# Moving one constant and padding it, so that every tile read by TensorE starts at a multiple of 1024 (or 512) bytes

## The chip, the cores and the metric

The kernel runs on one core of a Trainium2 chip. The metric is the device time of one launch in microseconds (us); lower is better. The engines are named as in the profile: PE is TensorE (its weight loads are shown apart as PEld), DVE is VectorE, ACT is ScalarE, POOL is GpSimd, SP is SyncE, which here only issues DMAs. SBUF is the on-chip memory; an address in it is counted in bytes within a partition.

## The reference

There are 128 samples `x[b]` of 128 tokens by 512 features in float32, and one adjacency matrix `adj` of 128 by 128.

```
# layer 0
A = adj @ x ;  C = A + b ;  out = max over n of relu(A + (C - A))      # b per token
x = layernorm(x + out)
# layer 1: attention with 8 heads of 64, masked where adj == 0
q, k, v = x @ w_qkv
p = softmax(mask(q k^T / 8)) ;  o = (p v) @ w_proj + b_proj
x = layernorm(x + o + layernorm(o) * gamma + beta)
```

## The kernel before

The samples go in 32 groups of four. Products in which precision matters (the `dense` products of q, k and v, and the projection `po`) are done with fp32r operands: each operand is split into a high part, a low part and a difference (`x_h`, `x_l`, `x_d` for the activations, `w_h`, `w_l`, `w_d` for the qkv weights, `p_h`, `p_l`, `p_d` for the projection, `oh`, `ol`, `od` for the attention output). One product is 12 matmuls of 128 x 512: eight by `product` (L342, L343) and four by `product_d` (L350). A group has 12 `dense` products, called (g, j): j = 0 to 3 are v of the four samples, with the activations stationary and the weights moving; j = 4 to 11 are q and k, with the weights stationary and the activations moving. It also has four projections ('o', b), with `oh`, `ol`, `od` stationary and `p_h`, `p_l`, `p_d` moving. So there are 16 x 12 = 192 fp32r matmuls for a group. In the last eight projections the attention output is written into the then unused storage of `w_h`, `w_l`, `w_d`, so there the stationary operand lies in the weight tiles.

The other products are plain float32: `conv` (L186, `adjT` stationary, the sample `xt` moving), `scores` (L397), `attend` (L477, which reads the transposed weights `eT` and `v`).

Around the products DVE splits (L294, L296), adds the `product_d` parts (L381, L523), masks scores (L413) and normalizes softmax (L440); ACT does the exponentials (L431), copies two 16-bit planes of the softmax (L446) and of the normalized sample (L277), squares (L529); POOL makes differences (L308), the residual (L500, L501, L518) and the small arithmetic of the norms (L535, L536, L541, L544, L250). A transposition goes through DRAM: the planes are written (L450, L279) and read back by a transposing DMA into `eT` (L455) or `xT` (L283). SP issues nearly all DMAs from one queue, in order.

The order on every engine is fixed beforehand: each step gets a place by hand-set offsets (the table `O`), the steps are sorted by place, and each engine runs its own in that order and waits on semaphores. The order in a steady group on PE is: dense 4 and 5, two convs, dense 6, 8, 7, 11, 10, 9, then attend and scores, dense 0, po 0, dense 1, po 1, scores and attend, dense 2, dense 3, po 2, two convs, po 3.

Where a tile lies follows from the order in which the pools ask for it. The constant pool comes first: four small constants of the framework end at byte 16,512, then `b0_sb`, `ident`, `adjT`, `mask`, the nine weight tiles, `gamma_sb`, `bias_sb`, `beta_sb`, `mhalf` and `square`, each rounded up to 32 bytes. The pools for samples, groups and work follow without gaps. All tiles in them are multiples of 1024 bytes, down to the small statistics at the end.

Of the kernel before, what the change touches and what calls it, by code (L numbers as in the profile page):

```python
# [8 lines left out]
FP = mybir.dt.float32  # L9
# [17 lines left out]
def tile_adj_resnorm_d2(  # L27
# [39 lines left out]
    P = 128  # L67
    assert T == P and D == 512 and B % 4 == 0
    G = 4
# [6 lines left out]
    const = ctx.enter_context(tc.tile_pool(name="const", bufs=1))  # L76
# [15 lines left out]
        xs[b] = xt  # L92


    adj_sb = work.tile([P, D], FP, tag="xh", name="adj_sb")[:, :P]
    nc.scalar.dma_start(adj_sb, adj)
    b0_sb = const.tile([P, 1], FP, name="b0_sb")
# [67 lines left out]
    gamma_sb = const.tile([P, D], FP, name="gamma_sb")  # L165
    bias_sb = const.tile([P, D], FP, name="bias_sb")
    beta_sb = const.tile([P, D], FP, name="beta_sb")
    mhalf = const.tile([P, G], FP, name="mhalf")
    nc.vector.memset(mhalf, -0.5)
    square = const.tile([P, D], mybir.dt.bfloat16, name="square")  # L170

# [727 lines left out]
```

## Time and profile before

| what | value |
|---|---|
| median of 3 runs | 1971.6 us (1968.35 to 1975.02) |
| span of the profiled execution | 1967.2 us |
| PE busy, matmuls | 1872.0 us, 95% |
| DVE, ACT, POOL busy | 84%, 79%, 63% |
| TensorE clock granted, mean | 0.989 |
| from one steady group to the next (start of dense 4 of group 16 to that of group 17) | 974.67 to 1033.57, 58.90 us |

The profile gives the profiled execution by its span, from the first instruction to the last; its own time around the span is not given, and the median of the runs is 4.4 us above the span. In timelines a row has the start, the duration, engine, source line, operation, output and inputs, and the count if several are merged; a bracket gives idle time before it and what ended it. Ends of matmuls are modelled, so a row's duration is longer than its share of the stream; the distance from one start to the next is what a matmul costs there. Queue rows of SP (SPq) tell when a DMA was issued, not how long it ran.

### The profile page before, as it was taken

What the parts mean: (1) busy time and instruction counts of PE and PEld (TensorE: products, weight loads), DVE (VectorE), ACT (ScalarE), POOL (GpSimd) and SP (SyncE); (2) the same over time, 40 slices, a digit from 0 to 9 for tenths busy, and PEclk for the clock granted to TensorE, in tenths of its full rate; (3) what the DMA queues carried; (4) which work ended last, traced back from release to release, by engine and by line L of the source; (5) the groups of instructions that cost most, each with busy time, mean ns of one, the idle gap of its engine ahead of it and who ended that gap; (6) DMA issues with size and microseconds to landing.
All of it is one profiled execution on the core that took longest, in us unless ns stands there. A gap on an engine that the chain in (4) does not pass through costs nothing.

```text
span 1967.2 us, 33044 instructions
## 1 busy us (share of the span) xinstructions
PE 1872.0 (95%) x10569; PEld 1438.1 (73%) x10569; DVE 1648.1 (84%) x2585; ACT 1547.6 (79%) x3926; POOL 1246.0 (63%) x1935
## 2 busy tenths in 40 slices
PE   7799999999999999999999999999999999999995
PEld 4677777777777777777777777777777777777774
DVE  7778888888888888888888888888888888888875
ACT  4688878788878788878788878788878788878764
POOL 3256666666666666666666666666667666667667
PEclk9899999999999999999999999999999999999997
DMA  4366565666565666555666555766555666555641
GB/s 130 102 156 163 152 157 147 175 172 164 152 159 147 172 172 162 153 158 149 173 172 166 151 156 147 175 171 166 151 160 145 173 172 164 153 156 146 154 114 52
DMA packets 486141, 302.92 MB, mean 154 GB/s; under 512 B 399440, under 2 KB 403664, under 8 KB 485968
## 3 DMA queue, kind: packets, MB, share of 16 engines
q1 hardware_dynamic: 485104, 299.70, 57.2%
q8 instruction: 84, 1.38, 0.3%
q10 hardware_dynamic: 864, 1.12, 0.2%
q14 instruction: 89, 0.73, 0.1%
HBM read 72.16 MB, written 131.07 MB: 103 GB/s over the span
## 4 chain that ended last, share of the span: by engine, by line
PE 70%; POOL 11%; DVE 9%; issue 5%; ACT 3%; DMA 3%; SPq 0%; POOLq 0%; ACTq 0%; DVEq 0%
POOL x_d L308 5%; PE psc L397 5%; PE pav L477 5%; PE pa L186 3%; POOL od L308 2%; DMA eT<-rows 2%; DVE x_l L296 1%; DVE v L381 1%; POOL sum L536 1%; DVE xh L294 1%; ACT oh L303 1%; DVE o L523 1%; DVE o L548 1%; DVE o L509 1%; ACT x_h L303 1%
## 5 line engine op out<-in xcount | busy, mean ns | idle before, releaser
L431 ACT ACTIVATE e<-e,nmax 128x128 f32<-128x128 f32 x1016 | 393.1, 389 | 62.5 <-DVE nmax L422 62.5
L446 ACT COPY planes<-e 128x2048 uint16<-128x2048 uint16 x124 | 234.7, 1893 | 21.6 <-DVE e L440 21.5
L529 ACT ACTIVATE square<-o,sum 128x512 bf16<-128x512 f32 x256 | 183.1, 715 | 63.8 <-DVE o L523 62.8
L535 POOL TENSOR_SCALAR sum<-sum 128x1 f32<-128x1 f32 (+1 forms) x287 | 58.3, 203 | 269.8 <-ACT square L529 256.6
L501 POOL TENSOR_TENSOR xb<-xb,beta_sb 128x512 f32<-128x512 f32 x128 | 210.6, 1646 | 10.7
L308 POOL TENSOR_TENSOR x_d<-x_h,x_l 128x512 fp32r<-128x512 f32 x97 | 125.7, 1310 | 134.6 <-DVE x_l L296 74.9
L536 POOL TENSOR_TENSOR sum<-sum,mhalf 128x1 f32<-128x1 f32 (+1 forms) x287 | 181.1, 631 | 23.9
L431 ACT ACTIVATION_READ_ACCUMULATOR e<-e,nmax 128x1 f32 x1016 | 190.9, 188 | 0.0
L518 POOL TENSOR_TENSOR xb<-xb,o 128x512 f32<-128x512 f32 x125 | 164.6, 1317 | 4.9
L440 DVE TENSOR_TENSOR e<-e,sums 128x1024 f32<-128x1024 f32 x128 | 162.3, 1268 | 4.4
L548 DVE SCALAR_TENSOR_TENSOR o<-o,sum,gamma_sb 128x512 f32<-128x512 f32 x128 | 99.3, 776 | 76.5 <-POOL xb L518 72.9
L413 DVE SCALAR_TENSOR_TENSOR e<-psc,mask 128x1024 f32<-128x1024 f32 x127 | 151.8, 1216 | 3.3 <-ACT planes L446 2.7
L422 DVE TENSOR_REDUCE nmax<-e 128x8 f32<-128x1024 f32 x127 | 153.5, 1209 | 0.1
L477 PE MATMUL pav<-eT,v 128*64 128x128 f32 x2048 | 140.1, 280 | 11.4 <-DMA eT<-rows 5.4
L556 ACT ACTIVATE o<-o,sum 128x512 f32<-128x512 f32 x128 | 103.1, 807 | 54.6 <-POOL sum L544 54.6
L397 PE MATMUL psc<-qkT 64*128 64x128 f32 x2048 | 141.8, 284 | 2.5 <-DVE qkT L381 2.5
L500 POOL TENSOR_SCALAR xb<-xb,sum 128x512 f32<-128x512 f32 x128 | 120.8, 944 | 35.3 <-DMA xb<-in_x_dram 33.9
L397 PEld LDWEIGHTS psc<-qkT 64*128 64x128 f32 x2048 | 123.4, 189 | 25.9 <-issue 21.4
L259 ACT ACTIVATE xt<-xt,sum 128x512 f32<-128x512 f32 x127 | 102.4, 806 | 46.3 <-POOL sum L250 45.2
L477 PEld LDWEIGHTS pav<-eT,v 128*64 128x64 f32 x2048 | 110.8, 137 | 37.3 <-issue 15.4
L277 ACT COPY xplanes<-xt 128x1024 uint16<-128x1024 uint16 x124 | 129.7, 1046 | 5.1 <-DMA rowsx<-xplanes 1.2
L186 PE MATMUL pa<-xt,adjT 128*128 128x512 f32 x256 | 123.6, 607 | 6.9 <-ACT v L325 3.5
(4668 smaller groups left out, 5606.3 us busy)
## 6 DMA issues: line engine op xcount, KB each, us to landing
rows<-planes SPq DMA_DIRECT2D x124, 512.0 KB, 3.3
xt<-in_x_dram SPq DMA_DIRECT2D x128, 256.0 KB, 3.0
xb<-in_x_dram SPq DMA_DIRECT2D x128, 256.0 KB, 3.0
out_dram<-o SPq DMA_DIRECT2D x128, 256.0 KB, 2.8
rowsx<-xplanes SPq DMA_DIRECT2D x124, 256.0 KB, 2.4
wraw<-in_L_gnn_w_qkv_dram SPq DMA_DIRECT2D x8, 256.0 KB, 2.9
xT<-rowsx SPq DMA_TRANSPOSE x124, 3.6
eT<-rows SPq DMA_TRANSPOSE x124, 4.7
```

Source lines behind the costliest of these rows:

```text
L186: nc.tensor.matmul(pa[b], adjT, xs[b], start=True, stop=True)
L308: engine.tensor_tensor(fd, fh.bitcast(FP), fl.bitcast(FP), op=ALU.subtract)
L397: nc.tensor.matmul(psc[:, s, hp, :], qkT[hs, hp, i, :], qkT[hs, KC + hp, i, :], start=not with_mask, stop=not with_mask or hp == HP - 1,)
L422: nc.vector.tensor_reduce(nmax, src, AX.X, ALU.max, negate=True)
L431: nc.scalar.activation(e[:, j, :], src[:, j, :], AF.Exp, bias=nmax[:, j : j + 1], scale=1.0 if src is e else scale, accum_out=sums[:, j : ...
L440: nc.vector.tensor_tensor(e, e, sums[:, :, None].to_broadcast([P, H, P]), op=ALU.mult)
L446: nc.scalar.copy(planes, e.rearrange("p h m -> p (h m)").bitcast(U16).rearrange("p (m s) -> p s m", s=2),)
L477: nc.tensor.matmul(pavs[b][s * HD : (s + 1) * HD, hp, :], v[:, h * HD : (h + 1) * HD], eT[:, s * HP + hp, :], start=True, stop=True,)
L501: nc.gpsimd.tensor_tensor(xbs[b], xbs[b], beta_sb, op=ALU.add)
L518: engine.tensor_tensor(xbs[b], xbs[b], os[b], op=ALU.add)
L529: nc.scalar.activation(square, x, AF.Square, bias=s[:, 0:1], scale=-float(D), accum_out=s[:, 1:2],)
L536: nc.gpsimd.tensor_tensor(s, s, mhalf[:, :n], op=ALU.pow)
```

## The change

`mhalf`, a constant of four floats a partition that POOL uses as an exponent, is taken from the constant pool first and with 88 floats (352 bytes) instead of four (which took 32 with rounding); the code uses the first four as before. Nothing else is changed: the same instructions stand in the same order on every engine, with the same waits.

```
+    mhalf = const.tile([P, 88], FP, name="mhalf")[:, :G]
     adj_sb = work.tile([P, D], FP, tag="xh", name="adj_sb")[:, :P]
     ...
     beta_sb = const.tile([P, D], FP, name="beta_sb")
-    mhalf = const.tile([P, G], FP, name="mhalf")
     nc.vector.memset(mhalf, -0.5)
```

The addresses that follow from it:

| tile | start before | its remainder by 1024 and by 64 | start after | remainder by 1024 |
|---|---|---|---|---|
| `ident` | 16,544 | 160, 32 | 16,896 | 512 |
| `adjT` | 17,056 | 672, 32 | 17,408 | 0 |
| `w_h` | 18,080 | 672, 32 | 18,432 | 0 |
| `w_l`, `w_d`, `p_h`, `p_l`, `p_d` | 42,656 and on | 672, 32 | 43,008 and on | 0 |
| `gamma_sb`, `bias_sb`, `beta_sb` | 116,384 and on | 672, 32 | 116,736 and on | 0 |
| the sample tiles `xt` | 123,584 and on | 704, 0 | 123,904 and on | 0 |
| `x_h`, `x_l`, `x_d` | 131,776 and on | 704, 0 | 132,096 and on | 0 |
| `v`, `qkT`, `eT`, `oh`, `ol`, `od`, and the other work tiles | 156,352 and on | 704, 0 | 156,672 and on | 0 |

The weights and other constants move up by 352 bytes and everything behind them by 320. Slices of a tile that TensorE takes start at multiples of 512 bytes within it. So before, an operand in the weight tiles starts 32 bytes past a multiple of 64, and one in the group and work tiles at a multiple of 64; after, both start at multiples of 512. Among the group and work tiles the distances stay as they are.

## The prediction

> **What bounds the kernel now.** I read the page's first part and its chain first, then PE's timeline near the end and in a steady group, then the waits, and last the timelines of ACT, SP and DVE around the place where PE waits.
>
> ```profile
> span 1967.2 us, 33044 instructions
> ...
> PE 1872.0 (95%) x10569; PEld 1438.1 (73%) x10569; DVE 1648.1 (84%) x2585; ACT 1547.6 (79%) x3926; POOL 1246.0 (63%) x1935
> ...
> PE 70%; POOL 11%; DVE 9%; issue 5%; ACT 3%; DMA 3%; SPq 0%; POOLq 0%; ACTq 0%; DVEq 0%
> ```
>
> PE is busy 95% and holds 70% of the chain. The change touches no instruction, so it can only act on how long one takes, and the first question is whether any row depends on addresses. PE's timeline near the end has one that does. There the projection of sample 120 follows a dense product without a stop, and its stationary operand lies in the weight tiles:
>
> ```profile
> 1892.13 0.40 PE L342 MATMUL pm_(31, 1)_19611<-w_h,x_h 128*128 128x512 f32 x1
> ...
> 1893.99 1.10 PE L350 MATMUL pd_(31, 1)_19612<-w_d,x_d 128*128 128x512 f32 x4
> 1894.93 0.39 PE L342 MATMUL pm_('o', 120)_19626<-p_h,w_h 128*128 128x512 f32 x1
> ...
> 1896.74 1.07 PE L350 MATMUL pd_('o', 120)_19627<-p_d,w_d 128*128 128x512 f32 x4
> ```
>
> From 1892.13 to 1894.93 twelve matmuls start: 233 ns each. Their operands are 32 bytes apart modulo 64 (weights at 672 modulo 1024, activations at 704 or 192). From 1894.93 to 1896.74 eight start: 226 ns each. Their operands are both 672 or 160 modulo 1024, so equal modulo 64. Shape, type and count are the same, and the step changes with the first matmul of the new kind. Taking all of the trace's steps under 245 ns by this distance, at least 8 matmuls after the last stop, those 32 apart stand at 231 to 235, mean 233.3, in over 4,000 cases; those 0 apart at 226 and 227 as a rule, in some 25. All of the latter are near the end. It is not the idleness there: dense products at 1907, with no DMA in flight, still step by 231 and 235. Just after a stop the 0-apart ones lose the advantage for a while: the first four average 231.5, the next four 229.
>
> **The change, part by part.** The memory set and the pow that use `mhalf` keep size and order: nothing. The plain float32 products have no such excess to lose:
>
> ```profile
> 1027.56 1.88 PE L186 MATMUL pa<-xt,adjT 128*128 128x512 f32 x4
> ```
>
> Four of them in 1.88 us, of which one takes 0.59: (1.88 - 0.59) / 3 = 430 ns from start to start, for two passes each. One pass at full clock is 213 (rows at half clock, around 1913 us, step by 427 for a single one). Its operands are 32 apart today, and it pays only some 3 ns for two passes. Scores and attend read tiles whose distance stays. So does everything that DVE, ACT and POOL read, but for mask, gamma, bias and beta; there the add of beta (L501, 32 apart) comes down to 1.28 us in the steady group, as the add of `o` (L518, 0 apart) with 1.29, so I take 0 for these.
>
> That leaves the 6,120 fp32r matmuls. The last eight projections, 96, are 0 apart already; 6,024 change. After it all distances are 0 or 512 modulo 1024, as in the rows of sample 120, so each should go from 233.3 to 226.7: 6.6 ns. If all of it reached the end it would be 6,024 x 6.6 = 40 us. It cannot: before 114 us and after 1888 us other engines hold the chain, and a steady group has a stretch from the last matmul of dense 3 to po 3 in which POOL holds it, with 24 fp32r matmuls inside (PE idles 1.02 us there, below). For 30 groups 30 x 168 x 6.6 = 33 us is the most.
>
> Here a rule weighs against the change. The Trainium skill, "SBUF — State Buffer", section "Who interferes with whom", gives PE two independent read ports, one for the moving operand and one for the weight load, and says that PE never waits on anyone; by that the distance of the two starts could not matter and the sum would be 0. The rows above differ by 7 ns, and the rows decide.
>
> **Where the gain stops.** The steady group's turning points:
>
> ```profile
> 1015.46 2.20 PE L477 MATMUL pav<-eT,v 128*64 128x128 f32 x32
> ...
> 1023.45 1.10 PE L350 MATMUL pd_(16, 3)_10518<-w_d,x_d 128*128 128x512 f32 x4
> 1024.66 0.50 PE L342 MATMUL pp_('o', 62)_10543<-p_h,oh 128*128 128x512 f32 x1
> ...
> 1032.32 1.20 PE L350 MATMUL pd_('o', 63)_10606<-p_d,od 128*128 128x512 f32 x4 [1.02 <-POOL od L308]
> 1033.57 0.47 PE L342 MATMUL pp_(17, 4)_10644<-x_h,w_h 128*128 128x512 f32 x1
> ```
>
> ```profile
> PE pav L477 <- DMA eT<-rows: 5.2, 10, 0.9
> ```
>
> The second line is from PE's waits between 300 and 1800 us. In 10 of some 26 groups PE already arrives too early at the fourth attend and waits for the transposed `eT`; in the group shown it arrives about when `eT` lands. So PE may be faster in the 42 us from dense 4 to that attend (about 160 of the 192 matmuls) and only wait longer for `eT`, unless `eT` comes earlier too. ACT and SP tell when it comes:
>
> ```profile
> 1000.14 0.81 ACT L259 ACTIVATE xt<-xt,sum 128x512 f32<-128x512 f32 x1 [1.44 <-POOL sum L250]
> ...
> 1010.35 1.05 ACT L277 COPY xplanes<-xt 128x1024 uint16<-128x1024 uint16 x1
> ```
>
> ```profile
> 1011.42 0.34 SPq L279 DMA_DIRECT2D rowsx<-xplanes  x1
> 1011.86 2.13 SPq L455 DMA_TRANSPOSE eT<-rows  x1
> ```
>
> ```profile
> 1023.39 1.22 DVE L413 SCALAR_TENSOR_TENSOR e<-psc,mask 128x1024 f32<-128x1024 f32 x1
> ...
> 1026.83 0.69 DVE L296 TENSOR_TENSOR ol<-pav,xh_('o', 63)_10562 128x512 fp32r<-128x512 f32 x1 [1.03 <-PE pp_('o', 62)_10543 L343]
> ```
>
> `eT` of the fourth attend is issued at 1011.86, because SP is in order and its queue stood behind the write of the sample planes at 1011.42, which waits for ACT's copy of 1010.35; with the median 4.7 us from issue to landing (the page's DMA issues) it lands at 1016.56, just when that attend starts. ACT works without a break from 1000.14 to there, and started on POOL's norm. Followed further back in the same timelines: POOL from 983.2, on the residual's sample loaded (3.0 us) from 980.25; DVE from 967.9 to 980.2; and DVE's split at 967.9, like the one at 1026.83, waits for the last main matmul of po 2, which reads the single buffer `ol`. So there is a second circle of one group's length, through DVE, SP, POOL, DVE, ACT, POOL, ACT, SP and PE, and of PE's fp32r matmuls it holds only dense 2, dense 3 and eight of po 2: 24 + 8 = 32. They give 32 x 6.6 = 0.21 us a group. Besides, po 2 starts at 1024.66, while dense 3 ends at 1023.45 + 4 x 0.233 = 1024.38: 0.28 us, spent on DVE's masking (1023.39 + 1.22 = 1024.61), which frees the PSUM buffer. That row stands behind DVE work that PE feeds, so up to 0.28 can go too. Between 0.21 and 0.49 us a group I take the middle, 0.35: 30 x 0.35 = 10.5 us. The rest of PE's 1.27 us turns into a longer wait for `eT`. The span becomes 1967.2 - 10.5 = 1956.7, and with the 4.4 us by which the median of the runs stands above the span, 1961.
>
> DMA ends change alignment too, from 192 to 0 modulo 256. No row shows an aligned SBUF end, so its price is open: none at the low end; at the high end a tenth of the three transfers in the circle, 3.0, 2.4 and 4.7 us, 1.0 us a group, as packets of 2048 and 4096 bytes take 84 and 159 ns in the trace, 9 of the 84 beyond the 75 by which they differ. Since packets of 4 bytes need 9 ns as well, I take 0. The Trainium skill, "DMA: Bandwidth & Descriptors", section "How a descriptor splits into AXI transactions", lets a descriptor that is not 256-byte aligned start at the boundary below; by that some transfers would shorten, which no row here confirms.
>
> **The rivals.** *The steps fall and the gain passes through.* If ACT's and DVE's part of the circle shortens, because PE's earlier products or shorter DMAs reach it, the bound is PE's own: up to 33 us, 1939; typically half, 1950. For it: ACT has waits on PE in its row before 1000. Against: the 11 us of unbroken ACT before the issue of `eT`.
>
> *The steps do not fall, or nothing reaches the end.* The fast rows are few and late; the distance could be a proxy for something else there. Then 1971.6. Against: the change within one run of PE at 1894.93.
>
> *Slower.* With all starts at 0 modulo 1024 the two streams may run into each other in the same place all the time, as the 0-apart rows do just after a stop, where single steps reach 236. If that state lasts, each of 6,024 matmuls costs 236 - 233.3 = 2.7 ns more; nothing hides added PE time, since PE arrives with `eT` today: 16 us, 1988. It decides from 1 ns a matmul on, 6 us. Against: in the late rows this state is over after some ten matmuls.
>
> **How the numbers follow.** The second circle holds: 0.57, 1955 to 1966, forecast 1961. Passing through: 0.15, 1939 to 1955. No change that reaches the end: 0.17, 1966 to 1977. Slower: 0.11, around 1988. The range from 1941 to 1973 takes the first case, most of the second and third, and leaves out 0.2. Faster by over 0.3% (6 us, about what a measurement of this kernel can tell from no change) is the first two, 0.72; within it 0.17; slower 0.11.
>
> **What would show it.** In the profile after: twelve dense matmuls in 2.72 us in place of 2.80 in long unbroken rows; conv at 429 ns and scores and attend unchanged; PE's busy share below 95%; PE's wait for `eT` above 5.2 us, toward 0.5 us or more a group; from dense 4 to dense 4 about 58.55 us. The prediction is wrong in its first step if the dense step stays at 233, and in its second if the step falls and the period goes below 58.2 or stays at 58.9.

## The result: no change that can be measured, and the profile after

| | before | after |
|---|---|---|
| median | 1970.3 us (4 runs, 1968.35 to 1975.02) | 1973.2 us (4 runs, 1968.14 to 1975.14) |
| ratio after to before | | 1.0014, 95% interval 0.9992 to 1.0035 |
| span of the profiled execution | 1967.2 us | 1973.3 us (its own time 1975.14) |
| PE busy | 1872.0 us | 1846.8 us |
| period: median distance from dense 4 to dense 4, groups 3 to 28 | 58.89 us | 58.93 us |

The forecast was 1961, range 1941 to 1973: the time is just outside it. PE lost 25 us of work, and nothing of it reached the end. Periods and counts of groups below are over these 26 groups, numbered as in the profile. The first part of the page after the change, and its chain:

```profile
span 1973.3 us, 33044 instructions
...
PE 1846.8 (94%) x10569; PEld 1439.5 (73%) x10569; DVE 1674.1 (85%) x2585; ACT 1550.1 (79%) x3926; POOL 1274.4 (65%) x1935
...
PE 55%; POOL 15%; DVE 10%; ACT 9%; issue 6%; DMA 5%; SPq 0%; POOLq 0%; DVEq 0%; ACTq 0%
```

PE's share of the chain fell from 70% to 55%, POOL's and ACT's rose. And DVE and POOL, whose instructions are the same as before, are busy for 26 and 28 us more. PE's timeline at the place where the prediction read the two steps:

```profile
1899.84 0.39 PE L342 MATMUL pm_(31, 1)_19611<-w_h,x_h 128*128 128x512 f32 x1
...
1902.56 0.39 PE L342 MATMUL pm_('o', 120)_19626<-p_h,w_h 128*128 128x512 f32 x1
```

Twelve dense matmuls now take 2.72 us, 227 ns each (2.80 and 233 before). Over the whole trace the step is 226.85 ns on average from the eleventh matmul after a stop on. The four of conv still take 1.88 us. So the first step of the prediction came true to within 0.2 ns. Its second step did too in its direction; PE's waits from 300 to 1800 us:

```profile
PE pav L477 <- DMA eT<-rows: 22.5, 20, 2.5
PE pav L477 <- ACT xt L259: 7.0, 6, 1.5
```

Together 29.5 us against 6.4 before (the 5.2 shown above and 1.2 for `xt`), 0.9 us a group more. The shorter period that should have come with it (58.55) did not. Where it went is seen around the softmax product L440 of the second sample, the last of the four L440 in the stretch from dense 4 to dense 4 (the expectation of a run below calls it the third sample's). DVE's and POOL's timelines of the same group, before:

```profile
1013.54 0.69 DVE L509 SCALAR_TENSOR_TENSOR o<-pm_('o', 61)_10405,bias_sb 128x512 f32<-128x512 f32 x1 [0.99 <-PE pm_('o', 61)_10405 L343]
...
1017.44 1.44 DVE L440 TENSOR_TENSOR e<-e,sums 128x1024 f32<-128x1024 f32 x1
...
1021.05 0.75 DVE L523 SCALAR_TENSOR_TENSOR o<-o,sum,xb 128x512 f32<-128x512 f32 x1
```

```profile
1017.19 1.52 POOL L301 TENSOR_SCALAR x_h<-xh 128x512 fp32r<-128x512 f32 x1
1018.78 1.30 POOL L518 TENSOR_TENSOR xb<-xb,o 128x512 f32<-128x512 f32 x1
```

and after:

```profile
1020.36 0.69 DVE L509 SCALAR_TENSOR_TENSOR o<-pm_('o', 61)_10405,bias_sb 128x512 f32<-128x512 f32 x1 [0.84 <-PE pm_('o', 61)_10405 L343]
...
1024.39 1.23 DVE L440 TENSOR_TENSOR e<-e,sums 128x1024 f32<-128x1024 f32 x1
...
1027.79 1.58 DVE L523 SCALAR_TENSOR_TENSOR o<-o,sum,xb 128x512 f32<-128x512 f32 x1
```

```profile
1024.60 2.40 POOL L301 TENSOR_SCALAR x_h<-xh 128x512 fp32r<-128x512 f32 x1
1027.08 1.75 POOL L518 TENSOR_TENSOR xb<-xb,o 128x512 f32<-128x512 f32 x1
```

The group shown starts at 974.67 before and at 982.19 after. DVE waits for PE shortly ahead of L440 (at L509, for the main product of po 1), so it takes PE's lead over: its rows stand 0.5 to 0.8 us earlier in the group than before. POOL's L301 moves by only 0.1 us, since the operations before it follow ACT's square (L529). Before, POOL began 0.25 us ahead of L440; after, DVE begins 0.21 us ahead of L301. That turns the order. POOL's L301 now ends 1.4 us after L440 does, nearly its whole length of before, and takes 2.40 in place of 1.52. The add behind it (L518) comes late, is drawn out to 1.75 and meets DVE's L523, which takes 1.58 in place of 0.75. At the end of L523 DVE's lead is gone (it ends 0.06 us later in the group than before), L413 and po 2 start where they did, and so does the next group. The groups of instructions between 300 and 1800 us show that it is so in every group; before:

```profile
L523 DVE SCALAR_TENSOR_TENSOR o<-o,sum,xb 128x512 f32<-128x512 f32 x101 | 88.0, 871 | 8.0 <-POOL sum L541 0.5
```

```profile
L301 POOL TENSOR_SCALAR x_h<-xh 128x512 fp32r<-128x512 f32 x26 | 42.2, 1624 | 2.2
```

and after:

```profile
L523 DVE SCALAR_TENSOR_TENSOR o<-o,sum,xb 128x512 f32<-128x512 f32 x101 | 107.5, 1064 | 8.0 <-POOL sum L541 0.5
```

```profile
L301 POOL TENSOR_SCALAR x_h<-xh 128x512 fp32r<-128x512 f32 x26 | 61.4, 2363 | 2.2
```

In 23 of 26 groups of before POOL was first; after, DVE is first in all 26. The other three groups of before (3, 11 and 24) show the price with no edit at all. POOL was late there and DVE came first; L301 takes 2.40 to 2.59 us in them, L523 1.58 or 1.59, and the groups take 59.53 to 59.56 us, 0.65 more than the median. (POOL's lateness itself may have a part in that.) DVE and POOL in group 24 of before:

```profile
1489.24 1.22 DVE L440 TENSOR_TENSOR e<-e,sums 128x1024 f32<-128x1024 f32 x1
...
1492.64 1.58 DVE L523 SCALAR_TENSOR_TENSOR o<-o,sum,xb 128x512 f32<-128x512 f32 x1
```

```profile
1489.44 2.40 POOL L301 TENSOR_SCALAR x_h<-xh 128x512 fp32r<-128x512 f32 x1
```

### The profile page after: what moved, and what is told of

The parts are those of the page before. It is cut to its first block, busy times and chain, and to the rows that moved or that the text cites. A ratio compares the mean times of both kernels' runs of the same rounds, so it can differ in the third digit from the quotient of the medians.

```text
span 1973.3 us, 33044 instructions
## 1 busy us (share of the span) xinstructions
PE 1846.8 (94%) x10569; PEld 1439.5 (73%) x10569; DVE 1674.1 (85%) x2585; ACT 1550.1 (79%) x3926; POOL 1274.4 (65%) x1935
## 4 chain that ended last, share of the span: by engine, by line
PE 55%; POOL 15%; DVE 10%; ACT 9%; issue 6%; DMA 5%; SPq 0%; POOLq 0%; DVEq 0%; ACTq 0%
POOL x_d L308 5%; PE psc L397 4%; PE pav L477 4%; DMA eT<-rows 4%; ACT e L431 2%; PE pa L186 2%; POOL od L308 2%; POOL sum L536 2%; POOL xb L501 2%; DVE x_l L296 1%; POOL xb L518 1%; ACT xplanes L277 1%; POOL xb L500 1%; DVE xh L294 1%; ACT xt L259 1%
## 5 line engine op out<-in xcount | busy, mean ns | idle before, releaser
L529 ACT ACTIVATE square<-o,sum 128x512 bf16<-128x512 f32 x256 | 182.9, 714 | 65.9 <-DVE o L523 64.9
L518 POOL TENSOR_TENSOR xb<-xb,o 128x512 f32<-128x512 f32 x125 | 175.1, 1401 | 4.9
L548 DVE SCALAR_TENSOR_TENSOR o<-o,sum,gamma_sb 128x512 f32<-128x512 f32 x128 | 99.3, 776 | 76.1 <-POOL xb L518 71.1
L440 DVE TENSOR_TENSOR e<-e,sums 128x1024 f32<-128x1024 f32 x128 | 158.2, 1236 | 4.4
L413 DVE SCALAR_TENSOR_TENSOR e<-psc,mask 128x1024 f32<-128x1024 f32 x127 | 152.0, 1217 | 3.4 <-ACT planes L446 2.7
L523 DVE SCALAR_TENSOR_TENSOR o<-o,sum,xb 128x512 f32<-128x512 f32 x128 | 132.9, 1038 | 10.8 <-POOL sum L536 0.9
```

The lines of the kernel that those rows point to most:

```text
L413: nc.vector.scalar_tensor_tensor(e, pscs.pop(b).rearrange("p s a m -> p (s a) m"), scale, mask_b, op0=ALU.mult, op1=ALU.add,)
L440: nc.vector.tensor_tensor(e, e, sums[:, :, None].to_broadcast([P, H, P]), op=ALU.mult)
L518: engine.tensor_tensor(xbs[b], xbs[b], os[b], op=ALU.add)
L529: nc.scalar.activation(square, x, AF.Square, bias=s[:, 0:1], scale=-float(D), accum_out=s[:, 1:2],)
```

## The theory and its rivals

*Theory.* PE's gain becomes a lead of DVE. In the group shown POOL began 0.25 us ahead, so from about 0.25 us on the lead turns the order in which L440 and POOL meet; the two then hold each other up ("collision" and "block" below), and this eats the lead. *Rival 1:* the circle through `eT`, as the prediction had it, is all there is, and it leaves nothing. *Rival 2:* the new places of the tiles themselves slow DVE and POOL (or the transfers) by what they gain for PE.

## Experiments

**All operands 0 apart modulo 64, but nothing at a multiple of 1024.** `mhalf` first, not padded:

```
+    mhalf = const.tile([P, G], FP, name="mhalf")       # 704 modulo 1024 for all
     ...
-    mhalf = const.tile([P, G], FP, name="mhalf")
```

> mhalf comes first in the constant pool but without the padding: all operands of TensorE are 0 apart modulo 64, while they start at 704 modulo 1024 (no multiples of 1024 or 256). Theory (only the distance modulo 64 counts for the fp32r step, and the gain is lost where DVE and POOL collide around L301, L440, L518, L523): dense steps settle at 226 to 227, PE busy near 1847, L301 on x_h near 2.3 us a piece, the add of L523 near 1.04, and the time is that of the changed kernel, 1968 to 1978. Rival (the start at a multiple of 1024, or the DMA alignment that comes with it, is what slows the other engines and eats the gain): the steps fall as well, but L301 stays near 1.67 and L523 near 0.88, and the time is 1955 to 1965. Rival (multiples of 1024 are needed for the faster step): steps stay at 233 and PE busy at 1872.

Measured: 1975.8 us, ratio 1.0025 (1.0014 to 1.0037); step 226.85; L301 2.36 us, L523 1.06; DVE first in all groups. It is the changed kernel again. So multiples of 1024 and the DMA alignment have no part in it, in the gain or in the loss. With 12 runs against 23 the interval lies above 1: here the change costs a little, some 5 us.

**Only `p_*` moved.** `mhalf` unpadded stands just ahead of `p_h`, so that only the projections get the short step.

> Only p_h, p_l, p_d move (by 32 bytes), so only the projections are 0 apart from oh, ol, od; the dense products stay 32 apart. Theory (the lead of DVE flips the order in which L440 and POOL's L301 meet, from a lead of about 0.25 us on): the lead at L440 comes from po 0 and po 1 alone, 24 x 6.6 = 0.16 us, too little to flip it; L301 on x_h stays near 1.67 us, L523 near 0.88, and the time is 1962 to 1971, the 8 to 12 matmuls of po 2 and the 24 being kept in part. Rival (nothing that PE gains can reach the end, since the circle through eT holds it): 1968 to 1974 with L301 and L523 as before. Rival (the moved constants slow DVE or POOL by their place): L523 and L301 change with no lead to explain it.

Measured: 1970.2 us, ratio 0.9997 (0.9985 to 1.0009); projections 228 on average, dense 233.3; L301 1.65, L523 0.88; POOL first in 22 of 26 groups. The lead was too small to turn the order, as expected; but the gain that the theory hoped for is not to be seen (period 58.86), and the time fits the first rival as well.

**Only `w_*` moved.** `mhalf` first, and two dummies of 32 bytes ahead of `p_h` and of `square`.

> The reverse of the run with only p_* moved: the nine... that is, w_h, w_l, w_d are 0 apart from x_h, x_l, x_d modulo 64, while p_h, p_l, p_d stay 32 apart from oh, ol, od (dense products at 226 to 227, projections at 233). Theory (a lead of DVE of about 0.25 us or more at L440 flips the order at L440 and L301): the dense products give the lead, so L301 on x_h goes to about 2.3 us a piece, L523 to about 1.05, and the time is 1968 to 1978, although three quarters of the matmuls are faster. Rival (the place of p_* and not the lead is what changes L301 and L523): L301 stays at 1.6, L523 at 0.88. Rival (the circle through eT alone bounds): L301 and L523 unchanged, time 1963 to 1969.

Measured: 1975.6 us, ratio 1.0012 (0.9998 to 1.0027); L301 2.49, L523 1.04; DVE first in 25 of 26 groups, period 59.14. The collision came with the dense products' lead, while `p_*` stood as far from its partners as before. But the steps are not those expected: in this layout the activations are 64 bytes above the weights, and the step is 229.0 where the activations move through the array and 233.3 where the weights do. That is taken up below.

**The lead without the layout.** The strongest test: in the layout of before, DVE gets its lead by leaving out most of one add shortly ahead of L440 (the second part of dense 1).

```
+        n = 64 if j == 1 else D
-        nc.vector.tensor_tensor(dst, dst, pps.pop((g, j))[1], op=ALU.add)
+        nc.vector.tensor_tensor(dst[:, :n], dst[:, :n], pps.pop((g, j))[1][:, :n], op=ALU.add)
```

> The layout of before; DVE's add of the second part of dense 1 (L381 with j = 1) is done on 64 of 512 columns only, so that part of v is left out. This takes about 0.5 us of work from DVE just before the softmax product L440 of the third sample (0.68 us become about 0.15), which is the lead that the faster steps of PE give in the changed layout, without touching PE. Theory (the order at L440 and L301 flips with the lead): L301 on x_h goes from 1.6 to about 2.35 us, L523 from 0.87 to about 1.05, the period stays at 58.8 to 59.0 and the time at 1966 to 1977, although work was taken away. Rival (it is the layout and not the lead that lengthens L301 and L523): both stay, and the half microsecond is kept in part: 1955 to 1967.

Measured: 1970.4 us, ratio 0.9998 (0.9989 to 1.0007). The same two groups of instructions (the edit shifts lines behind it by one):

```profile
L524 DVE SCALAR_TENSOR_TENSOR o<-o,sum,xb 128x512 f32<-128x512 f32 x101 | 107.3, 1063 | 8.0 <-POOL sum L542 0.5
```

```profile
L301 POOL TENSOR_SCALAR x_h<-xh 128x512 fp32r<-128x512 f32 x26 | 61.6, 2370 | 2.2
```

No tile has moved and PE is as slow as before (1872.2 us busy), and yet both rows are those of after. The period is 59.08, a little above what was expected and 0.19 longer than before, although each group has 0.46 us less work on DVE. Rival 2 falls with this run as the cause of these rows.

**POOL's add made short, in both layouts.** `residual_o` works on 64 of 512 columns.

> The layout of before, but POOL adds o to xb (L518) on 64 of 512 columns only, so most of the residual is left out of the output; it shortens the POOL operation that meets L523 from about 1.3 us to about 0.3. Theory: the collision at L518 and L523 shrinks, L523 comes down toward 0.75 us a piece (3.0 us a group in place of 3.5), and the time is 1930 to 1962. Rival (the circle through eT alone sets the period): 1964 to 1974, since POOL's add lies beside it.

> The layout of the changed kernel with the same shortened add (L518 on 64 of 512 columns, most of the residual left out). Theory (collision): with the collision small, PE's faster steps are kept: 10 to 30 us faster than the same edit in the layout of before. Rival (the circle through eT alone): 6 to 15 us faster than that. Rival (the layout slows other engines by as much as it speeds PE): within 5 us of it.

Measured: 1958.8 us and 1942.0 us; the new layout is 16.8 us faster where POOL's add cannot stand in L523's way. L301 is still 2.35 us there and DVE still first in all groups; but L523 is 0.84. So it is the second meeting, L518 with L523, that costs the time. By the medians alone rival 1 (6 to 15 us) is not excluded, as the intervals leave some 5 us either way. The periods are 58.86 and 58.04, 0.82 us a group where the second circle was to leave at most 0.49. But that does not exclude it either: the shortened add is itself a link of that circle (at 989.80 of the profile before, DVE's L548 had waited 2.29 us for POOL's L518), so the circle is shorter in both of these runs. In the layout of before the period does not change (58.86), so the 11 us there come from irregular groups and the ends, not from a collision in every group.

**`x_h` of each group's first sample on ACT, in both layouts.** This takes L301 off POOL, so that L518 is over before L523.

```
-         'h': [1, 0, 0, 0, 0, 1, 0, 0],
+         'h': [0, 0, 0, 0, 0, 1, 0, 0],
- 'x_high': [-2.23, 2.47, -9.83, 1.18],
+ 'x_high': [3.5, 2.47, -9.83, 1.18],
```

> The layout of before, but the x_h of each group's first sample is made by ACT after the oh of the third projection (L303, about 0.63 us) and not by POOL (L301, 1.6 us). POOL's next add (L518) then comes earlier and clears the place where L523 read both of its inputs. Theory (collision): little to gain here, since in this layout L518 and L523 met by only half a microsecond: 1955 to 1972. Rival (the circle through ACT and eT alone bounds): ACT's extra 0.63 us a group lies behind its copy of the planes, so no change: 1967 to 1974.

> The same edit in the layout of the changed kernel. Theory (collision): L518 runs before L523, which comes back to 0.9 us a piece or less, PE's faster steps are kept in good part, and the time is 10 to 30 us below the same edit in the layout of before: 1935 to 1960. Rival (the circle through eT alone bounds): 6 to 15 us below it. Rival (what PE gains cannot reach the end, or the layout slows other engines): within 5 us of it.

Measured: 1993.3 us in the layout of before, ratio 1.0095 (1.0073 to 1.0116), which no theory had; 1958.3 us in the new one, ratio 0.9931 (0.9905 to 0.9957). The time of the second is in the range of the theory; the difference of 35 us is in no range, because of the first. DVE's and POOL's timelines of the latter:

```profile
1018.21 1.23 DVE L440 TENSOR_TENSOR e<-e,sums 128x1024 f32<-128x1024 f32 x1
...
1021.60 0.75 DVE L523 SCALAR_TENSOR_TENSOR o<-o,sum,xb 128x512 f32<-128x512 f32 x1
```

```profile
1018.34 2.24 POOL L518 TENSOR_TENSOR xb<-xb,o 128x512 f32<-128x512 f32 x1
```

L518 loses against L440, by 0.13 us, but is over at 1020.58, and L523 is back at 0.75: the period is 58.31. The miss in the layout of before is the same thing with the other sign. There L518 now starts where L301 did, just ahead of L440:

```profile
1265.60 2.29 DVE L440 TENSOR_TENSOR e<-e,sums 128x1024 f32<-128x1024 f32 x1
```

```profile
1265.53 1.28 POOL L518 TENSOR_TENSOR xb<-xb,o 128x512 f32<-128x512 f32 x1 [0.29 <-DVE o L523]
```

Here 70 ns decide: L440 takes 2.29 in place of 1.23. In 22 groups of this run POOL was first, and their median is 59.76; in 4 DVE was, and theirs is 58.78. With DVE first in both layouts, the new one is 58.78 - 58.31 = 0.47 us a group better (25 of its 26 groups have DVE first). This is a rough figure, with four groups on one side, of what PE's steps are worth when nothing else turns.

**POOL's two operations exchanged, in the new layout.** `x_high` of the first sample at 2.5, still on POOL: L518 comes before L301.

> The layout of the changed kernel, with POOL's two operations in the other order: the add of L518 for the group's second sample comes before x_h of the next group's first sample (L301). Theory (collision): L518 now meets L440 and is over before L523, but L301 moves to the place where L523 runs; L301 reads one SBUF tile and should cost L523 less than the add did: L523 at 0.8 to 1.0 us a piece, time 1945 to 1965. Rival (any POOL operation there blocks L523 as much): 1968 to 1978 as the changed kernel. Rival (the circle through eT alone): 1960 to 1968.

Measured: 1960.2 us, ratio 0.9934 (0.9913 to 0.9955), period 58.45. The two groups of instructions:

```profile
L523 DVE SCALAR_TENSOR_TENSOR o<-o,sum,xb 128x512 f32<-128x512 f32 x102 | 86.3, 846 | 8.1 <-POOL sum L541 0.5
```

```profile
L301 POOL TENSOR_SCALAR x_h<-xh 128x512 fp32r<-128x512 f32 x26 | 40.3, 1551 | 1.8
```

The time lies just inside the last rival's range too, so the rows must decide: both are back at about their lengths of before, and rival 1 by itself gives no reason why the exchange should win anything. Same instructions, same layout, only two of them in the other order on POOL: 13 us below the changed kernel. (The exchange alone was not run in the layout of before.) Some price is left: L548 waits beside L301 now (1.06 in place of 0.74 in the group looked at).

**One wait more taken away.** Besides `x_h` on ACT, POOL makes `od` of the fourth projection before `x_d` (`o_d[3]` from 10.06 to 8.0).

> The changed layout with x_h of each group's first sample on ACT, as before, and besides POOL makes od of the fourth projection (L308) before x_d of the next group's third sample, not after it. PE's wait for that od, about 0.85 us a group, should go. Theory (with the collision out of the way what PE gains in the tail of the group reaches the end): 10 to 25 us below the run without this second edit: 1933 to 1950. Rival (the wait for eT takes it over in full): 1952 to 1962.

Measured: 1952.5 us, ratio 0.9908 (0.9894 to 0.9921), period 58.03: faster than both kernels, and the fastest here in which nothing is left out. PE's wait for `od` is gone, but dense 4 now waits 1.0 us a group for DVE's L523 of the third projection, so about a third of the 0.85 us came through. The rival had it right.

**Which distance counts.** A dummy of 32 bytes behind the constants puts all operands 32 past a multiple of 64, 64 apart:

> mhalf stays where it was and a dummy of 32 bytes behind it moves everything that follows by 32 bytes: the weights start at 672 and the other operands at 736 modulo 1024, all 32 past a multiple of 64. Theory (the distance of the two starts modulo 64 counts, not the start itself): dense steps at 226 to 227, PE busy near 1848, time as with the changed kernel, 1968 to 1979. Rival (operands must start at multiples of 64): steps at 233 or more, PE busy at 1870 or above.

Measured: 1975.1 us, ratio 1.0022 (1.001 to 1.0033), L523 1.04: the collision again. The step is 229.2 ns with the activations moving (64 above the weights) and 233.3 with the weights moving (64 below). So "0 modulo 64" is not the rule, and the odd start is not the cause either, since the run with only `w_*` moved has the same 229.0 and 233.3 at multiples of 64. Two runs with 128 and 256 bytes between weights and activations followed:

> mhalf first and unpadded, and 128 bytes of padding behind the constants: weights at 704 modulo 1024, the other operands at 832, so 128 apart, and all at multiples of 64. The run with all operands 64 apart had 229 (moving operand 64 above) and 233 (64 below), so a distance of 0 modulo 64 is not enough. If the distance counts modulo 128: dense steps at 226 to 227, PE busy near 1847, time as with the changed kernel (1970 to 1978). If it counts modulo 256, 512 or 1024: 229 to 233, PE busy 1855 to 1872, and the time 1968 to 1978 all the same, since what PE gains is lost at L440 and L301.

> The same with 256 bytes of padding: weights at 704, the other operands at 960 modulo 1024, 256 apart. If the distance counts modulo 128 or 256: dense steps at 226 to 227, PE busy near 1847. If it counts modulo 512 or 1024: 229 to 233, PE busy 1855 to 1872. The time is 1968 to 1978 in either case.

PE's row of the page, 128 apart and then 256 apart:

```profile
PE 1867.1 (95%) x10569; PEld 1438.3 (73%) x10569; DVE 1649.3 (84%) x2586; ACT 1547.5 (79%) x3926; POOL 1248.2 (64%) x1935
```

```profile
PE 1848.4 (94%) x10569; PEld 1440.2 (73%) x10569; DVE 1670.1 (85%) x2586; ACT 1549.5 (79%) x3926; POOL 1272.3 (64%) x1935
```

At 128 apart the step is 232.7, at 256 apart 226.9. So the short step comes at 0 and at 256, not at 32 or 128, and at 64 about two thirds of the gain comes, one way round only. The times: 1968.3 (ratio 0.9986, 0.997 to 1.0003), L301 1.68, POOL first in 21 of 26 groups; and 1974.8 (1.0009, 0.9991 to 1.0028), L301 2.36, DVE first in all. With the long step the old order stays in most groups, with the short one the new order holds in all: the pair repeats before and after at new addresses.

## Why the prediction was wrong

**The step of PE: right for this change.** 233.3 ns became 226.85 and PE's work fell by 25 us. Its stated reason, the distance modulo 64, was read from only two kinds of distance and does not hold at 64 and 128.

**The DMA term, taken at 0: right.** Packets of 2048 and 4096 bytes take 84 and 159 ns after as before (medians between 300 and 1800 us), so packets of these sizes did not shorten with their alignment.

**The second circle: right in kind, and not far off in size.** The prediction took 0.35 us a group, bounds 0.21 to 0.49; the two runs with `x_h` on ACT, compared in groups of the same order, give about 0.47. PE's wait for `eT` grew as it said. ("About 160 of the 192 matmuls" ahead of the fourth attend are 144, twelve products; the sum does not use that count.)

**The step that failed: "Between 0.21 and 0.49 us a group I take the middle, 0.35".** What came was -0.04 (58.89 to 58.93). The step left the durations of DVE's and POOL's instructions as they were, as if a lead changed only when they run. But two of them overlap, and how long they take depends on who starts first. The rows of before had it: this L440 stood at 1.44 where the other three of the group take 1.22 to 1.25; POOL had begun 0.25 us earlier; and DVE, unlike POOL, hung on PE just before. The price is 58.93 - 58.31 = 0.62 us a group, the changed layout with and without the collision (with the cost of the edit itself in it). It takes all of the 0.35 and of the 0.47, and it agrees with the 0.65 of the three groups of before in which DVE was first.

The Trainium skill, "SBUF — State Buffer", section "Who interferes with whom", says of DVE instructions with two SBUF inputs and GpSimd instructions that read SBUF that they contend, and: "Issue order, not op shape, decides who blocks." The rows agree on the order: leads of 0.07 to 0.25 us decided here. By it L440, L523 and L548 were among the candidates. How long the second one is held up is another matter; the rows on that stand in the last section.

**A second loss that the sum had at nothing.** "The rest of PE's 1.27 us turns into a longer wait for `eT`" was costed at zero. Mostly it is. But where `eT` comes late, PE now stands still long enough for its clock to drop. PE's timeline and the windows of the profile after (columns: stretch, its length, PE busy, granted clock, DMA share, GB/s):

```profile
787.61 1.09 PE L477 MATMUL pav<-eT,v 128*64 128x128 f32 x16 [2.30 <-DMA eT<-rows]
```

```profile
785.90:788.90 3.00, 1.29 (x20) 0.99 0.98 188
788.90:791.90 3.00, 3.00 (x19) 0.50 0.70 226
791.90:794.90 3.00, 3.00 (x14) 0.94 0.79 208
```

After 2.30 us of waiting the clock is at 0.50 for some 3 us. Groups by the same windows:

```profile
743.90:805.40 61.50, 58.25 (x328) 0.97 0.59 154
805.40:864.30 58.90, 56.66 (x328) 1.00 0.60 161
```

Three groups of the profile after are such (60.8, 61.5 and 61.5 in place of 58.9: 7 us), none of the profile before between 150 and 1800 us. This is about the 6.1 us by which the 26 groups together are longer in the profile after; the 3.6 us that its start loses, its tail gains.

**The offset.** The 4.4 us "by which the median of the runs stands above the span" were mostly scatter of the runs. After, the execution's own time is 1.84 us above its span.

**The rivals.** "No change that reaches the end" (0.17) named the outcome, with 1966 to 1977, but for another reason: the steps fell, and the gain reached as far as L440. "Slower" had a mechanism on PE that did not occur.

## What to carry to other kernels

Before you credit a faster engine, look at whose start times it moves, and whether those stand within half a microsecond of a start on the other side of a shared resource: there a lead can turn an order, and the durations of unchanged instructions change with it. An instruction that takes 1.44 us where its like take 1.23 marks such a place, and a short retiming (here exchanging two POOL operations) has to go with the change before its gain shows. For fp32r matmuls of this shape, start the moving and the stationary operand a multiple of 256 bytes apart: 0 and 256 gave the short step here.

## What the hardware showed that was not expected

- The step of an fp32r 128 x 512 matmul depends on the distance between its two operands' starts: 226.9 ns at 0 and at 256 bytes, 232.7 at 128, 233.3 at 32 either way, 229.0 with the moving operand 64 above and 233.3 with it 64 below. Distances are meant up to multiples of 512, by which the slices step here. Why the step depends on them is open.
- The block between DVE and POOL is not the same from both sides. L440 (two SBUF inputs, 1.23 us as a rule) takes only 1.44 us when a POOL scaling of 1.52 us (L301, one input) began 0.25 us earlier, and 1.61 when it began 0.08 earlier (group 12 of before): lead and loss add up to under half a microsecond, so by these two rows L301 holds L440 up only in its first part. A POOL add of 1.28 us (L518, two inputs) that began 0.07 earlier costs L440 1.06 us (2.29), nearly the whole add. Where L440 is first, either POOL operation waits until about its end.
- Standing still can lower PE's clock sooner than thought. In all profiles of this study PE waited 1.8 us or longer 30 times between 150 and 1800 us; after 19 of these the clock fell to half for some 3 us (once for longer); the shortest such wait was 1.81 us. After waits of 1.5 to 1.8 us it never did. The Trainium skill, "TensorE: Matmul & The Clock Gate", section "What's actually happening", puts the fall after an idle window of about 3.4 us; here 1.81 us was enough, and what decided among the longer ones is open: one of 2.69 us had no such fall.
- A late `eT` (6.2 to 6.9 us from issue to landing, 4.5 to 4.7 in the median) occurs up to four times between 150 and 1800 us of a run, in either layout (6.3 at most before, 6.5 after). Why some transfers are late was not tried.
